# RGCN edge stages: sums carried across tiles, an empty tile between relations, and a scatter-add that waits for the one two ahead

## The chip, the cores and the metric

The kernel runs on one core of a Trainium2 chip. The metric is the device time of one execution in microseconds; lower is better. The engines are TensorE (PE, with its weight loads as PEld), VectorE (DVE), ScalarE (ACT), GpSimd (POOL) and SyncE (SP), which issues the plain DMAs. Indirect DMAs (gathers, scatters, scatter-adds) are issued by GpSimd.

## The reference

There are 10000 nodes with 512 features and 5000 edges. The output is made by four blocks with residual sums: a two-layer relational graph convolution (RGCN), a mixture-of-experts feed-forward block, a four-layer GINE network and a ternary feed-forward block. The change touches the first block alone:

```python
def rgcn_gate_layer(x, row, col, edge_type, basis, att, gate_w, root, bias):
    w = jnp.einsum('rb,bio->rio', att, basis)
    x_j = x[col]
    msgs = []
    for r in range(NUM_RELATIONS):
        gate = jax.nn.sigmoid(x_j @ gate_w[r, :, 0])
        msgs.append(gate[:, None] * x_j @ w[r])
    msg = jnp.where((edge_type == 0)[:, None], msgs[0], msgs[1])
    agg = jax.ops.segment_sum(msg, row, num_segments=x.shape[0])
    return agg + x @ root + bias
...
h = jax.nn.relu(rgcn_gate_layer(x, row, col, edge_type, basis1, att1, gate_w1, root1, bias1))
out = rgcn_gate_layer(h, row, col, edge_type, basis2, att2, gate_w2, root2, bias2)
```

`row` (the input `src`) is the node that an edge adds to, `col` (`dst`) the node whose features it reads; there are two relations and 30 basis matrices of 512x512.

## The kernel before

**Preparation.** `sort_edges` sorts the edges on the chip, once by relation and `src`, the node that an RGCN edge adds to (`by_src`, its table `by_src_d`), and once by `dst`, the node that a GINE edge adds to (`by_dst`). The sorted edges of `by_src` lie in 41 tiles (`RT`) of 128; the second relation starts at a tile's border. Beside the sort the node pass `rgcn_nodes1` normalizes all nodes, multiplies them by the root matrix and writes the result to `r1_d`. `relation_weights` adds the basis matrices up, on DVE (L637).

**Targets.** Within a tile several edges can have the same target. `equal_keys` (L212) compares a tile's 128 keys with each other, and `add_targets` keeps the target's row for the first edge of each key; the others get a spare row of their own behind the nodes (the last 128 rows of `r1_d` and `a2_d`). So a scatter-add never names a node twice. Two neighbouring tiles can name the same node, where a key's edges go over a border.

**The edge stages.** `rgcn_edges` runs twice over the tiles: stage 1 reads the normalized nodes and adds to `r1_d`, stage 2 reads `r1_d` through a ReLU and adds to `a2_d`. For each tile t:
- `fetch`: an indirect gather of 128 node rows into `x` (eight buffers), L614.
- `make_ready`: in stage 2 the ReLU on ACT (L665); two dot products with the gates on DVE (`prod`, L669); a sigmoid on ACT (`g`, L674); the choice by relation on DVE (`dots`, L675); a transpose of the keys on TensorE (`ps_k`, L680); then `same` on DVE (L682), a 128x128 matrix that is the gate where two edges have one key, and zero elsewhere.
- `add_up`: four products of `x` with `same` on TensorE (L689), which add the edges of each key and give the transposed sums; ACT copies them to `aT` (L693). Column j of `aT` is the sum for the key of edge j.
- `put`: the product of `aT` with the relation's weights (L703, eight TensorE instructions in the trace), whose place comes from a register; ACT copies it to `o` (three buffers, L708); GpSimd issues the scatter-add (L619) of `o` to the targets.

The loop runs these staggered, `FETCHED` = 6 and `READY` = 3. In turn i the order is: gather of tile i, `add_up` of tile i-5, `put` of tile i-6, `make_ready` of tile i-3, and then a piece of other work. That other work is the generator `placing` (`place_nodes`): it goes forward by one piece in every second turn of stage 1 and in each turn of stage 2, and ends in stage 2. The orders of PE, GpSimd, ACT and DVE in this loop are those of the code (`manual_schedule`); around it a scheduler decides. Scatter-adds of one stage name the same DRAM tensor, so each waits for the landing of the one before.

When stage 1 has landed, the gathers of stage 2 start; when stage 2 has landed, the first feed-forward block loads `r1_d` and `a2_d`.

`place_nodes` also holds the lines that find, for the sort by `dst`, whether a key goes on into the next tile (`ends`, `carried`); the GINE block carries its sums with them.

Of the kernel before, what the change touches and what calls it, by code (L numbers as in the profile page):

```python
# [8 lines left out]
F32 = mybir.dt.float32  # L9
BF = mybir.dt.bfloat16  # L10
F16 = mybir.dt.float16
I32 = mybir.dt.int32
AF = mybir.ActivationFunctionType
OP = mybir.AluOpType
# [3 lines left out]
P = 128  # L18
N = 10000
D = 512  # L20
KC = D // P
E = 5000
ET = 40
EP = E // ET
SENT = 30000.0
EDGE_SLOTS = ET * P
LO = 256
HI = (N + LO - 1) // LO
RT = ET + 1

PAIRS = [(p * 1024, 512) for p in range(N // 1024)] + [(N // 1024 * 1024, N % 1024 // 2)]
PT = 8
# [13 lines left out]
FETCHED, READY = 6, 3  # L46
# [23 lines left out]
def gnn_ffn_kernel(ctx: ExitStack, tc: tile.TileContext, I, out, dram):  # L70
    nc = tc.nc
# [6 lines left out]


    xn_d = dram("xn_d", [N, D])  # L80
    r1_d = dram("r1_d", [N + P, D])
    a2_d = dram("a2_d", [N + P, D])
    xf_d = dram("xf_d", [N + P, D])
    x2_d = dram("x2_d", [N + P, D])
    xg_d = dram("xg_d", [N, D])
# [41 lines left out]
    nc.vector.memset(eps_t, LN_EPS)  # L127

    def clear_spare(zero, d):
        nc.sync.dma_start(d[N:, :], zero)  # L130


    def rows_to(sb, d, b, store=False):
# [83 lines left out]
    def sort_edges(tag, key_d, partner_d, attr_d, table, wk, ps, keep, by_relation=False):  # L217
# [77 lines left out]
        if by_relation:  # L295

            first_r = wk.tile([P, P], F32, name="first_r")
            nc.vector.tensor_scalar(off[:, 1:2], ip, float(HI), None, op0=OP.is_lt)
            nc.vector.tensor_scalar(first_r, ones, off[:, 1:2], None, op0=OP.mult)
            ps_o = ps.tile([P, LO], F32, name="ps_s")  # L300
            nc.tensor.matmul(ps_o[:hr, :1], lhsT=first_r[:hr, :hr], rhs=total[:hr], start=True, stop=True)
            n_i = wk.tile([P, 3], I32, name="n_i")
            nc.vector.tensor_scalar(n_i[:hr, 0:1], ps_o[:hr, :1], float(P - 1), None, op0=OP.add)
            nc.vector.tensor_scalar(n_i[:hr, 1:2], n_i[:hr, 0:1], 7, None, op0=OP.logical_shift_right)
            nc.vector.tensor_scalar(n_i[:hr, 2:3], n_i[:hr, 1:2], 7, None, op0=OP.logical_shift_left)
            nc.vector.tensor_copy(off[:hr, 1:2], n_i[:hr, 2:3])
            nc.vector.tensor_sub(off[:hr, 1:2], off[:hr, 1:2], ps_o[:hr, :1])
            nc.vector.tensor_scalar(off[:hr, 2:3], ip[:hr], float(HI), None, op0=OP.is_ge)
            nc.vector.tensor_mul(off[:hr, 1:2], off[:hr, 1:2], off[:hr, 2:3])
            nc.vector.tensor_add(off[:hr, 0:1], off[:hr, 0:1], off[:hr, 1:2])  # L310
            nc.vector.tensor_copy(off[:1, 3:4], n_i[:1, 1:2])
            w_at = keep.tile([1, RT], I32, name=f"w_at_{tag}")
            nc.vector.tensor_scalar(
                w_at, irow[:1, :RT], off[:1, 3:4], float(KC * D), op0=OP.is_ge, op1=OP.mult
            )
            meta["w_at"] = w_at

            pad = wk.tile([P, RT + 1, 4], F32, name="pad")
            nc.vector.memset(pad, 0.0)
            nc.vector.memset(pad[:, :, 0], SENT)  # L320
            nc.sync.dma_start(table.rearrange("(p t) c -> p t c", p=P), pad)
# [47 lines left out]
        nc.vector.tensor_copy(gidx, srt[:, :, 1])  # L369
        return dict(meta, key=key, gidx=gidx, attr=srt[:, :, 2])  # L370

    def add_targets(meta, wk, ps, keep):

        key = meta["key"]
        first = wk.tile([P, RT], F32, name="before")
        equal_keys(key, RT, below, first, wk, ps)
        w = wk.tile([P, RT], F32, name="w_se")
        nc.vector.tensor_scalar(first, first, 0.0, None, op0=OP.is_equal)
        nc.vector.tensor_scalar(w, key, float(N), None, op0=OP.is_lt)
        nc.vector.tensor_mul(first, first, w)  # L380
        spare = wk.tile([P, RT], F32, name="spare")
        nc.vector.tensor_scalar(spare, ip.to_broadcast([P, RT]), float(N), None, op0=OP.add)
        nc.vector.tensor_sub(w, key, spare)
        nc.vector.tensor_mul(w, w, first)
        nc.vector.tensor_add(w, w, spare)
        sidx = keep.tile([P, RT], I32, name="sidx")
        nc.vector.tensor_copy(sidx, w)
        return dict(meta, sidx=sidx)

    def place_nodes(meta, wk, ps, keep):  # L390

# [6 lines left out]

        key = meta["key"]
        tno = irow[:, :ET]  # L400

        ends = wk.tile([P, 2, ET], F32, name="ends")
        for i, sel in enumerate((first_sel, last_sel)):
            ps_l = ps.tile([P, LO], F32, name="ps_s")
            nc.tensor.matmul(ps_l[:, :ET], lhsT=sel, rhs=key, start=True, stop=True)
            nc.vector.tensor_copy(ends[:, i], ps_l[:, :ET])
        carried = keep.tile([P, 4, ET], F32, name="carried")
        co, stays, passes, enters = (carried[:, i] for i in range(4))
        nc.vector.memset(carried, 0.0)
        nc.vector.tensor_tensor(co[:, : ET - 1], ends[:, 1, : ET - 1], ends[:, 0, 1:], OP.is_equal)  # L410
        nc.vector.tensor_scalar(stays, co, -1.0, 1.0, op0=OP.mult, op1=OP.add)

        nc.vector.tensor_tensor(passes, ends[:, 0], ends[:, 1], OP.is_equal)
        nc.vector.tensor_mul(passes, passes, co)
        nc.vector.tensor_mul(passes[:, 1:], passes[:, 1:], co[:, : ET - 1])
        nc.vector.tensor_sub(enters[:, 1:], co[:, : ET - 1], passes[:, 1:])
        yield

        ahead = wk.tile([P, ET], F32, name="ahead")
# [198 lines left out]
    def scatter_add(dst, idx, src):  # L618
        return nc.gpsimd.indirect_dma_start(  # L619
            out=dst, out_offset=bass.IndirectOffsetOnAxis(ap=idx, axis=0), in_=src, in_offset=None,  # L620
            compute_op=OP.add,
        )
# [17 lines left out]
    def rgcn_edges(tag, meta, src_d, relu, ws, gate_d, dst_d, beside, take):  # L640

        with ExitStack() as s:
            fix = s.enter_context(tc.tile_pool(name=f"re_fix_{tag}", bufs=1))
            wk = s.enter_context(tc.tile_pool(name=f"re_wk_{tag}", bufs=3))
# [6 lines left out]
            nc.vector.tensor_scalar(of_rel[:, :, 1], meta["attr"], 0.0, None, op0=OP.not_equal)  # L653
            w_all = ws.rearrange("p r w -> p (r w)")

            got, ready, sums = {}, {}, {}

            def fetch(t):
                got[t] = wk.tile([P, D], F32, name="x", bufs=FETCHED + 2)
# [2 lines left out]
            def make_ready(t):  # L662
                x, kt = got[t], meta["key"][:, t : t + 1]
                if relu:
                    nc.scalar.activation(x, x, AF.Relu)  # L665
                dots = wk.tile([P, RELATIONS], F32, name="dots")
                prod = wk.tile([P, D], F32, name="prod", bufs=2)
                for r in range(RELATIONS):
                    nc.vector.scalar_tensor_tensor(  # L669
                        prod, x, 1.0, gate[:, r * D : (r + 1) * D], op0=OP.mult, op1=OP.mult,  # L670
                        accum_out=dots[:, r : r + 1],
                    )
                g = wk.tile([P, RELATIONS + 1], F32, name="g")
                nc.scalar.activation(g[:, :RELATIONS], dots, AF.Sigmoid)  # L674
                nc.vector.scalar_tensor_tensor(  # L675
                    dots, g[:, :RELATIONS], 1.0, of_rel[:, t, :], op0=OP.mult, op1=OP.mult,
                    accum_out=g[:, RELATIONS:],
                )
                ps_k = pk.tile([P, P], F32, name="ps_k")
                nc.tensor.transpose(ps_k, kt.to_broadcast([P, P]), ident)  # L680
                same = wk.tile([P, P], F32, name="same", bufs=4)
                nc.vector.tensor_scalar(same, ps_k, kt, g[:, RELATIONS:], op0=OP.is_equal, op1=OP.mult)  # L682
                ready[t] = same

            def add_up(t):
# [6 lines left out]
                sums[t] = wk.tile([P, KC, P], F32, name="aT")  # L692
                nc.scalar.copy(sums[t], ps_a)  # L693

            def put(t):
                aT = sums.pop(t)
                w0 = nc.values_load(
                    meta["w_at"][:, t : t + 1], engines=(mybir.EngineType.PE,), min_val=0, max_val=KC * D,
                    skip_runtime_bounds_check_because="it is 0 or KC * D by the comparison that makes it",
                )  # L700
                ps_o = po.tile([P, D], F32, name="ps_o")
                for k in range(KC):
                    nc.tensor.matmul(  # L703
                        ps_o, lhsT=aT[:, k, :], rhs=w_all[:, bass.ds(w0 + k * D, D)],
                        start=k == 0, stop=k == KC - 1,
                    )
                o = wk.tile([P, D], F32, name="o")
                nc.scalar.copy(o, ps_o)  # L708
                scatter_add(dst_d, meta["sidx"][:, t : t + 1], o)

            E_ = mybir.EngineType
            with tc.manual_schedule(engines={E_.PE, E_.Pool, E_.Activation, E_.DVE}):
                for i in range(RT + FETCHED):
                    if i < RT:
                        fetch(i)
                    if i >= FETCHED - 1 and i - FETCHED + 1 < RT:
                        add_up(i - FETCHED + 1)
                    if i >= FETCHED:
                        put(i - FETCHED)
                    if READY <= i < RT + READY:  # L720
                        make_ready(i - READY)
                    if take(i):
                        next(beside, None)

# [1149 lines left out]
```

## Time and profile before

| | |
|---|---|
| median of 3 runs | 4619.68 us (4619.44 to 4631.54) |
| the profiled execution | 4620.11 us |
| its span, first to last instruction | 4618.3 us |
| mean granted TensorE clock | 0.937 |
| busy share PE / DVE / ACT / POOL | 87% / 61% / 37% / 34% |
| first gather of stage 1 | 534.3 us |
| first gather of stage 2 | 842.2 us |
| first load of the next block | 1096.2 us |
| scatter-adds | 41 in each stage, 1.58 us (median) each on GpSimd |

The times inside the span are read from the timeline. "Busy" is the time in which an engine ran instructions; a group's row gives the operation, output and inputs, the count, the busy time and the mean, and behind them the idle time before it with what ended it ("<-" names the releaser). A wait's row gives the total wait, the number of waits and the longest. The granted clock is in parts of full speed.

### The profile page before, as it was taken

The numbers are of one execution on the slowest core, as the hardware profiler recorded it, in microseconds if no ns is written. First come the engines' busy times: TensorE is split into PE (matmuls) and PEld (weight loads), VectorE is DVE, ScalarE is ACT, GpSimd is POOL, SyncE is SP. The second block draws the span as 40 slices with busy tenths as digits, with TensorE's granted clock in tenths as the row PEclk, the third lists the DMA queues.
The fourth block names the chain that finished last, engine by engine and source line by source line (L and its number), as shares of the span: only waits on it lengthen the run. The fifth ranks groups of instructions, "written<-read, shape, count | busy, mean of one in ns | idle before, by whom it ended". The sixth has DMA issues, their size and how long they took to land.

```text
span 4618.3 us, 42924 instructions
## 1 busy us (share of the span) xinstructions
PE 4021.0 (87%) x13624; PEld 2037.0 (44%) x13624; DVE 2799.6 (61%) x5886; ACT 1723.0 (37%) x3086; POOL 1548.1 (34%) x1124
## 2 busy tenths in 40 slices
PE   6799568897999953996879999999999999999997
PEld 3443234443444421443444545545455455544443
DVE  7888865553545455655765546654576455755776
ACT  4334112232333311114544523344233532335775
POOL 3434334342000034785563113311142111422443
PEclk9899789898989875998989999999999999999998
DMA  8777755456555422897621123102231012311332
GB/s 281 232 259 248 226 127 89 83 105 169 197 170 182 158 64 59 160 162 208 199 71 51 73 77 116 47 19 80 83 111 38 28 76 107 89 31 48 110 112 97
DMA packets 294560, 558.83 MB, mean 121 GB/s; under 512 B 41376, under 2 KB 72129, under 8 KB 293311
## 3 DMA queue, kind: packets, MB, share of 16 engines
q1 hardware_dynamic: 221072, 367.30, 23.5%
q0 software_dynamic: 73264, 188.79, 17.7%
q8 instruction: 111, 1.82, 0.2%
q14 instruction: 113, 0.93, 0.1%
HBM read 295.03 MB, written 260.95 MB: 120 GB/s over the span
## 4 chain that ended last, share of the span: by engine, by line
PE 37%; DVE 9%; DMA 3%; issue 2%; ACT 2%; POOL 1%; POOLq 0%; DVEq 0%; ACTq 0%; SPq 0%
PE ps_b L1340 15%; PE ps_d L1340 9%; PE ps_o L1646 5%; PE ps_e L1340 4%; PE ps_x L1482 2%; PE ps_x L1268 2%; DVE stats L1455 2%; DMA x<-xg_d,gpos 1%; DVE feat L1272 1%; DMA x_in<-x_d,node_at 1%; PE ps_q L1714 1%; DVE feat L1355 1%; DVE x L1257 1%; DVE t L1386 1%; POOL e L1261 1%
## 5 line engine op out<-in xcount | busy, mean ns | idle before, releaser
L1340 PE MATMUL ps_b<-feat,w 128*128 128x512 f32 (+1 forms) x1120 | 499.1, 588 | 6.9 <-ACT feat L1468 6.9
L1340 PE MATMUL ps_d<-feat,w_s 128*128 128x512 f32 (+1 forms) x1096 | 490.7, 584 | 2.2 <-DVE feat L1387 1.3
L1348 ACT ACTIVATE feat<-ps_b,cols 128x512 f32<-128x512 f32 (+1 forms) x300 | 204.1, 682 | 535.2 <-PE ps_b L1340 522.5
L1394 POOL TENSOR_TENSOR feat<-feat 128x1024 f32<-128x1024 f32 (+1 forms) x70 | 162.7, 2324 | 627.0 <-DVE feat L1393 601.9
L637 DVE SCALAR_TENSOR_TENSOR w<-basis,att,w 128x2048 f32<-128x2048 f32 x116 | 316.3, 2736 | 14.9 <-DMA basis<-in_L_gnn_basis 14.9
L742 PE MATMUL ps_o<-root,xT 128*128 128x512 f32 (+1 forms) x632 | 322.2, 622 | 0.0
L1409 POOL TENSOR_TENSOR feat<-feat,p 128x1024 f32<-128x1024 f32 (+1 forms) x66 | 166.7, 2525 | 449.2 <-ACT feat L1348 449.0
L1340 PEld LDWEIGHTS ps_b<-feat,w 128*128 128x128 f32 x1120 | 209.9, 192 | 240.8 <-issue 209.5
L703 PE MATMUL ps_o<-w,aT 128*128 x656 | 304.1, 608 | 0.0
L1484 DVE TENSOR_TENSOR x_rows<-ps_x,be 128x512 f32<-128x512 f32 (+1 forms) x237 | 157.5, 685 | 232.3 <-PE ps_x L1482 232.0
L918 PE MATMUL ps_n<-root,rT 128*128 128x512 f32 (+1 forms) x632 | 288.9, 613 | 0.0
L1340 PEld LDWEIGHTS ps_d<-feat,w_s 128*128 128x128 f32 x1096 | 198.4, 191 | 194.2 <-issue 173.0
L1340 PE MATMUL ps_b<-t,w_s 128*128 128x512 f32 (+1 forms) x560 | 253.2, 592 | 26.1 <-ACT feat L1348 26.1
L614 POOL DMA_INDIRECT x<-xg_d,gpos x160 | 175.6, 1098 | 260.8 <-PE ps_x L1268 50.8
L1340 PE MATMUL ps_e<-feat,w 128*128 128x512 f32 (+1 forms) x560 | 253.9, 592 | 9.3 <-DVE feat L1303 9.3
L1340 PE MATMUL ps_b<-feat,w_s 128*128 128x512 f32 (+1 forms) x560 | 250.0, 585 | 0.0
L1468 ACT ACTIVATE feat<-feat,bn_sm 128x512 f32<-128x512 f32 (+2 forms) x320 | 238.0, 808 | 3.6 <-DVE bn_sm L1446 3.6
L1455 DVE BATCH_NORM_STATS2 stats<-feat 128x6 f32<-128x512 f32 (+1 forms) x320 | 203.6, 667 | 41.4 <-POOL feat L1409 28.3
L1268 PEld LDWEIGHTS ps_x<-same,x 128*128 128x128 f32 x1280 | 165.5, 197 | 110.7 <-ACT x L1263 48.8
L1268 PE MATMUL ps_x<-same,x 128*128 128x128 f32 x1280 | 172.9, 284 | 46.8 <-ACT x L1263 33.1
L170 DVE BATCH_NORM_STATS2 ln_st<-x_in 128x6 f32<-128x512 f32 (+1 forms) x237 | 159.6, 683 | 63.0 <-DMA x_in<-x_d,node_at 59.0
L1263 ACT ACTIVATE x<-x 128x512 f32<-128x512 f32 x160 | 98.9, 628 | 242.4 <-DVE x L1257 174.2
(492 smaller groups left out, 7649.4 us busy)
## 6 DMA issues: line engine op xcount, KB each, us to landing
basis<-in_L_gnn_basis SPq DMA_DIRECT2D x60, 1024.0 KB
xg_d<-x_rows SPq DMA_DIRECT2D x234, 256.0 KB
xg_d<-x_in SPq DMA_DIRECT2D x39, 512.0 KB
x_in<-in_x SPq DMA_DIRECT2D x19, 1024.0 KB
a_d<-x_in SPq DMA_DIRECT2D x19, 1024.0 KB
xn_d<-xn SPq DMA_DIRECT2D x19, 1024.0 KB
r_d<-o_nodes SPq DMA_DIRECT2D x19, 1024.0 KB
r_in<-r_d SPq DMA_DIRECT2D x19, 1024.0 KB
```

What stands on the lines that cost most here:

```text
L614: return nc.gpsimd.indirect_dma_start(out=dst, out_offset=None, in_=src, in_offset=bass.IndirectOffsetOnAxis(ap=idx, axis=0))
L637: nc.vector.scalar_tensor_tensor(ws[:, r], tf, c, ws[:, r], op0=OP.mult, op1=OP.add)
L703: nc.tensor.matmul(ps_o, lhsT=aT[:, k, :], rhs=w_all[:, bass.ds(w0 + k * D, D)], start=k == 0, stop=k == KC - 1,)
L742: nc.tensor.matmul(ps_o[:n], lhsT=xT[:, k, a * P : a * P + n], rhs=root[:, k, :], start=k == 0, stop=k == KC - 1,)
L918: nc.tensor.matmul(ps_o[:n_], lhsT=rT[:, k, a * P : a * P + n_], rhs=root[:, k, :], start=k == 0, stop=k == KC - 1,)
L1268: nc.tensor.matmul(ps_a[:, k, :], lhsT=x[:, k * P : (k + 1) * P], rhs=same, start=True, stop=True)
L1340: nc.tensor.matmul(ps[fo], lhsT=A[a][:, k, fo * P : (fo + 1) * P], rhs=x[:, k, :], start=first and k == 0, stop=k == 1, skip_group_check=True,
L1348: nc.scalar.activation(dst[:, fo, :], ps[fo], func, bias=b, scale=scale)
L1409: (nc.vector if last else nc.gpsimd).tensor_tensor(b22, b22, p5, OP.add)
L1455: nc.vector.bn_stats(stats[:, k, 2 * p + j, :], big[:, k, s0 + j * w : s0 + (j + 1) * w])
L1468: nc.scalar.activation(hb, hb, AF.Relu, bias=sm[:, fo, 3:4], scale=sm[:, fo, 2:3])
L1646: nc.tensor.matmul(ps_o[:n_], lhsT=big[:, kc, t * P : t * P + n_], rhs=W2[kc], start=kc == 0, stop=kc == KC - 1,)
```

## The change

The scatter-add may now overlap the one before it, and for that two neighbouring tiles must not name the same node. Three things see to it:

- **A carry.** `carries` (moved out of `place_nodes`, with `ends_of`) makes for each tile two factors: `passes` (the key fills the tile and goes on) and `enters` (the first key came from the tile before and ends here). A new step `carry` in the loop takes the last column of `aT`, with what is passed on, as `acc`, and adds what the tile before left over to the first column of `aT`. `add_targets` now gives a key that goes on into the next tile the spare row instead of the node's.
- **An empty tile between the relations**, so that two tiles of one node in different relations don't lie side by side. `RT` becomes 42. Odd and even tiles have their own 128 spare rows, so `r1_d` and `a2_d` have 256, and `clear_spare` clears them in two DMAs.
- **The scatter-add** is declared free of the one before it; it still waits for the one two ahead.

GpSimd is also taken out of the loop's written order, and its instructions are placed by the scheduler.

```diff
-RT = ET + 1
+RT = ET + 2
...
-    r1_d = dram("r1_d", [N + P, D])
-    a2_d = dram("a2_d", [N + P, D])
+    r1_d = dram("r1_d", [N + 2 * P, D])
+    a2_d = dram("a2_d", [N + 2 * P, D])
...
     def clear_spare(zero, d):
-        nc.sync.dma_start(d[N:, :], zero)
+        for r0 in range(N, d.shape[0], P):
+            nc.sync.dma_start(d[r0 : r0 + P, :], zero)
...
-            nc.vector.tensor_scalar(n_i[:hr, 0:1], ps_o[:hr, :1], float(P - 1), None, op0=OP.add)
+            nc.vector.tensor_scalar(n_i[:hr, 0:1], ps_o[:hr, :1], float(2 * P - 1), None, op0=OP.add)
...
+    def ends_of(key, tiles, wk, ps):
+        ends = wk.tile([P, 2, tiles], F32, name="ends")
+        for i, sel in enumerate((first_sel, last_sel)):
+            ps_l = ps.tile([P, LO], F32, name="ps_s")
+            nc.tensor.matmul(ps_l[:, :tiles], lhsT=sel, rhs=key, start=True, stop=True)
+            nc.vector.tensor_copy(ends[:, i], ps_l[:, :tiles])
+        return ends
+
+    def carries(ends, tiles, keep, tag):
+        carried = keep.tile([P, 4, tiles], F32, name=f"carried_{tag}")
+        co, stays, passes, enters = (carried[:, i] for i in range(4))
+        nc.vector.memset(carried, 0.0)
+        nc.vector.tensor_tensor(co[:, : tiles - 1], ends[:, 1, : tiles - 1], ends[:, 0, 1:], OP.is_equal)
+        nc.vector.tensor_scalar(stays, co, -1.0, 1.0, op0=OP.mult, op1=OP.add)
+        nc.vector.tensor_tensor(passes, ends[:, 0], ends[:, 1], OP.is_equal)
+        nc.vector.tensor_mul(passes, passes, co)
+        nc.vector.tensor_mul(passes[:, 1:], passes[:, 1:], co[:, : tiles - 1])
+        nc.vector.tensor_sub(enters[:, 1:], co[:, : tiles - 1], passes[:, 1:])
+        return carried
...
         key = meta["key"]
+        both = wk.tile([P, RT], F32, name="key_rel")
+        nc.vector.tensor_scalar(both, meta["attr"], 0.0, 2.0 * SENT, op0=OP.not_equal, op1=OP.mult)
+        nc.vector.tensor_add(both, both, key)
+        ends = ends_of(both, RT, wk, ps)
+        carried = carries(ends, RT, keep, "s")
         first = wk.tile([P, RT], F32, name="before")
         equal_keys(key, RT, below, first, wk, ps)
         w = wk.tile([P, RT], F32, name="w_se")
+        nc.vector.tensor_tensor(w, both, ends[:, 1], OP.is_equal)
+        nc.vector.tensor_mul(w, w, carried[:, 0])
+        nc.vector.tensor_add(first, first, w)
...
-        nc.vector.tensor_scalar(spare, ip.to_broadcast([P, RT]), float(N), None, op0=OP.add)
+        nc.vector.tensor_scalar(odd, row_i[:, :RT], 1, None, op0=OP.bitwise_and)
+        nc.vector.tensor_copy(spare, odd)
+        nc.vector.tensor_scalar(spare, spare, float(P), ip, op0=OP.mult, op1=OP.add)
+        nc.vector.tensor_scalar(spare, spare, float(N), None, op0=OP.add)
...
+            acc = fix.tile([P, KC], F32, name="acc_0")
+            nc.vector.memset(acc, 0.0)
+            carry_on = {-1: acc}
...
+            def carry(t):
+                aT, last = sums[t], carry_on.pop(t - 1)
+                carry_on[t] = wk.tile([P, KC], F32, name="acc")
+                for dst, src, i in ((carry_on[t], P - 1, 2), (aT[:, :, 0], 0, 3)):
+                    nc.vector.scalar_tensor_tensor(
+                        dst, last, meta["carried"][:, i, t : t + 1], aT[:, :, src], op0=OP.mult, op1=OP.add
+                    )
...
-                scatter_add(dst_d, meta["sidx"][:, t : t + 1], o)
+                st = scatter_add(dst_d, meta["sidx"][:, t : t + 1], o)
+                if stores:
+                    tc.declare_no_dep(st.ins, stores[-1].ins, reason="they have different rows")
+                stores.append(st)
...
-            with tc.manual_schedule(engines={E_.PE, E_.Pool, E_.Activation, E_.DVE}):
+            with tc.manual_schedule(engines={E_.PE, E_.Activation, E_.DVE}):
...
                     if READY <= i < RT + READY:
                         make_ready(i - READY)
+                    if i >= FETCHED - 1 and i - FETCHED + 1 < RT:
+                        carry(i - FETCHED + 1)
                     if take(i):
                         next(beside, None)
```

The work beside comes behind the carry in a turn.

More of the change, by code (lines that the diff above doesn't have):

```diff
@@ L380, in add_targets @@
         nc.vector.tensor_mul(first, first, w)
+        odd = wk.tile([P, RT], I32, name="odd")
         spare = wk.tile([P, RT], F32, name="spare")
-        nc.vector.tensor_scalar(spare, ip.to_broadcast([P, RT]), float(N), None, op0=OP.add)
+        nc.vector.tensor_scalar(odd, row_i[:, :RT], 1, None, op0=OP.bitwise_and)
+        nc.vector.tensor_copy(spare, odd)
+        nc.vector.tensor_scalar(spare, spare, float(P), ip, op0=OP.mult, op1=OP.add)
+        nc.vector.tensor_scalar(spare, spare, float(N), None, op0=OP.add)
         nc.vector.tensor_sub(w, key, spare)
@@ L387, in add_targets @@
         nc.vector.tensor_copy(sidx, w)
-        return dict(meta, sidx=sidx)
+        return dict(meta, sidx=sidx, carried=carried)
     def place_nodes(meta, wk, ps, keep):
@@ L400, in place_nodes @@
         tno = irow[:, :ET]
[L402 to L416, printed above, removed]
+        ends = ends_of(key, ET, wk, ps)
+        carried = carries(ends, ET, keep, "d")
+        co = carried[:, 0]
         yield
@@ L654, in rgcn_edges @@
             w_all = ws.rearrange("p r w -> p (r w)")
-            got, ready, sums = {}, {}, {}
+            got, ready, sums, stores = {}, {}, {}, []
+            acc = fix.tile([P, KC], F32, name="acc_0")
+            nc.vector.memset(acc, 0.0)
+            carry_on = {-1: acc}
             def fetch(t):
```

## The prediction

> **What bounds the kernel now.** I began with the windows view, cut at the borders of the two edge stages. The page's chain of waits says nothing of them: its first piece, listed in order of time, starts at 2081 us. The edge stages run from the first gather (534.3 us) to the last landing of a scatter-add (1096.2 us), 562 us of the 4618.3 us span; before them lie the sort and the node pass, behind them the first feed-forward block.
>
> ```profile
> core 0: us, PE busy (x) PEld busy (x) DVE busy (x) ACT busy (x) POOL busy (x), PEclk, DMA share, GB/s
> ...
> 633.00:842.00 209.00, 173.30 (x653) 93.48 (x651) 99.04 (x377) 44.13 (x103) 89.18 (x66) 0.96 0.49 85
> ...
> 862.00:962.00 100.00, 100.00 (x411) 53.66 (x411) 64.05 (x236) 34.97 (x79) 47.98 (x36) 1.00 0.52 91
> 962.00:1050.00 88.00, 79.06 (x305) 42.06 (x304) 45.18 (x168) 26.89 (x60) 38.69 (x30) 0.96 0.57 110
> 1050.00:1097.00 47.00, 25.42 (x83) 12.60 (x82) 12.12 (x44) 7.62 (x16) 13.71 (x9) 0.78 0.42 63
> ```
>
> Each row is a stretch: its length, then each engine's busy time, the granted clock, DMA. TensorE is full for the first 100 us of stage 2, then less and less. Stage 2's waits tell why:
>
> ```profile
> DVE prod L669 <- ACT x L665: 54.7, 30, 4.3
> ACT o L708 <- DMA a_d<-o,sidx: 50.4, 20, 5.7
> ```
>
> The product of tile t+1 starts 5.12 us after that of tile t; a scatter-add starts only every 5.65 us, since each waits for the landing of the one before. The lag grows until the three buffers `o` are full (about 965 us); from there the scatter-adds set the pace. Here is one tile of stage 2 in the timeline while TensorE still sets it:
>
> ```profile
> 908.59 3.60 PE L703 MATMUL ps_o<-w,aT 128*128 x8
> ...
> 912.27 0.59 ACT L708 COPY o<-ps_o 128x512 f32<-128x512 f32 x1 [1.77 <-issue]
> ...
> 912.75 0.63 ACT L665 ACTIVATE x<-x 128x512 f32<-128x512 f32 x1
> ...
> 913.41 0.69 DVE L669 SCALAR_TENSOR_TENSOR prod<-x,gate 128x512 f32<-128x512 f32 x1 [1.35 <-ACT x L665]
> 913.60 0.30 PEld L703 LDWEIGHTS ps_o<-w,aT 128*128 128x128 f32 x2
> 913.71 3.60 PE L703 MATMUL ps_o<-w,aT 128*128 x8
> ...
> 914.15 0.69 DVE L669 SCALAR_TENSOR_TENSOR prod<-x,gate 128x512 f32<-128x512 f32 x1
> ...
> 914.94 0.20 ACT L674 ACTIVATE g<-dots 128x2 f32<-128x2 f32 x1 [1.56 <-DVE prod L669]
> ...
> 915.17 0.20 DVE L675 SCALAR_TENSOR_TENSOR dots<-g,of_rel 128x2 f32<-128x2 f32 x1 [0.33 <-ACT g L674]
> ...
> 915.49 0.41 DVE L682 TENSOR_SCALAR same<-ps_k,key_s,g 128x128 f32<-128x128 f32 x1
> ```
>
> Read it as a chain that starts at a product and ends at `same`: product, copy `o`, ReLU, two dot products, sigmoid, `dots`, `same`. ACT and DVE take their work in the written order, so `same` of tile i-3 comes 7 us behind the start of the product of tile i-6. This costs nothing today: `same` is read two turns later, and the next product (913.71) does not wait for it.
>
> **The change, part by part.**
>
> *The carry* is the part that decides. It adds two small DVE instructions to each tile, written behind `same` in the same turn, and they write the first column of `aT`, which the next turn's product reads. In the built order the product has a new wait on DVE, behind a register load; queued behind it on TensorE are the key transpose, the beside work and the next sums, and for these DVE waits in turn. So the slack of two turns is gone and the chain closes to a loop: product, `o`, (ReLU), dots, sigmoid, `same`, carry, next product.
> Stage 2, from the rows above: product to `o` 3.68, to ReLU 0.48, to the first `prod` 0.66, to the second 0.74, to sigmoid 0.79, to `dots` 0.23, to `same` 0.32, to the next DVE instruction 0.33 (at 905.21 `same` is followed at 905.54). The carry has no row; the nearest is `dots`, the same kind of instruction on 128x2, at 0.16 each, and small DVE work starts 0.1 apart, so 0.27 for both (bounds 0.2 and 0.5). From DVE's end to the weight load and the product 0.16 (DVE end 1054.76, weight load 1054.81, 0.11 more to the matmul). Sum 7.66; with the semaphore and register load now exposed I take 7.7 (7.5 to 8.0).
> Stage 1 has no ReLU and its dots run beside the product: 3.68 + 0.49 + 0.23 + 0.28 + 0.33 + 0.27 + 0.16 = 5.44, taken as 5.5. There the product now starts after 4.44 at best, 6.95 in turns where four tiles of `equal_keys` lie beside.
>
> *The scatter-add waits for the one two ahead.* This ends the 5.65 us pace: two in flight allow one per 2.8 us, and GpSimd needs 1.58 + 0.30 + 1.0 + 0.30 = 3.2 us per tile. But at 7.7 us per turn nobody waits for it; only the lag at the ends is won. Before, TensorE's last product of stage 2 ends at 1074.25 and the next block's first load starts at 1096.18; after, 0.08 + 0.59 + 0.28 + 5.5 = 6.45 us lie between. The weight preparation in that gap takes 10.8 us from 1074.3, and the next block's TensorE starts 7.3 us behind its first load (1103.49), so it stays covered. Were that cover gone, 4 us.
>
> *GpSimd's order is no longer written by hand.* Ten gathers now come before the first scatter-add and three more stay ahead throughout. A gather needs its buffer back from the sums of eight tiles ago, which TensorE does just before the product whose scatter-add stands behind that gather, so it holds nothing: 0.
>
> *One tile more* per stage (42), the empty one: one turn each.
>
> *Preparation* (0 to 534 us): 19 more DVE instructions, three TensorE ones; such rows take 0.17 to 0.19, so at most 3.6 us on a DVE that is 81% busy there. Two more clears on SP's queue (0.33 us each to issue, 0.25 MB each, 1 us at that stage's 250 GB/s) and three small column loads moved back. The order is otherwise nearly the old one. I take +3 (-3 to +6).
>
> *TensorE's clock.* The loop leaves a gap of about 2.5 us in each stage-2 turn (7.7 less the 5.12 of work). What a gap does, the timeline shows at 765 us:
>
> ```profile
> 762.77 0.27 PE L680 MATMUL ps_k<-ident,key_s 128*128 128x128 f32 x1
> 765.33 0.62 PE L488 MATMUL ps_s<-incl_p,less_next 40*41 40x256 f32 x2 [2.29 <-DVE less_next L486]
> ...
> 765.93 1.88 PE L689 MATMUL ps_a<-same,x 128*128 128x128 f32 x8
> 767.60 4.58 PE L703 MATMUL ps_o<-w,aT 128*128 x8
> ```
>
> After 2.29 us without work the product took 4.58 us, not 3.60, and the sums 1.88, not 1.06. The Trainium skill ("TensorE: Matmul & The Clock Gate", "HAM oscillation — how this bites in real kernels") gives the rule of no TensorE gaps above about 3.4 us; by it these gaps would cost nothing, and the sum below would be 15 smaller. By the row each can cost 1.0 (1.7 after the 3.97 us gap at 741, where the product took 5.29). Over the whole timeline 18 gaps of 2.0 to 2.5 us begin at full clock and 7 are followed by half clock (the clock's record moved 10.7 us earlier, where it fits the slow products). So 39 x 7/18 x 1.0 = +15; ends 0 and 39 x 1.7 = 66.
>
> **Sum for stage 1** (534 to 842.2). First six products, while DVE still builds weights: DVE is full in both, +5 (0 to 12). Then 16 short turns of 4.44 become 5.5: +17. Eighteen long ones get the carry's 0.25: +4.5. Turns with heavy DVE work beside (`passed` 3.5 and its reduction 3.4, the scans) used the lost slack: +8 (2 to 12). One turn more: +5.5. Lag at the end: 826.45 to 842.2 is 15.8, becomes 6.45: -9.3. Together +31.
>
> **Sum for stage 2** (842.2 to 1096.2, 254.0 us). After: 14.2 + 0.6 to the first product, 39 turns x 7.7 = 300.3, two last turns without dots 8.9, the last product 3.6, 6.45 to the landing: 334. So +80.
>
> All: 3 + 31 + 80 + 15 = +129. The profiled execution took 4620.1 us (span 4618.3 and 1.8 around it), the median of the runs is 4619.7. 4619.7 + 129 = 4749.
>
> **The rivals.**
> *The pace was the scatter-add's, and the carry hides* (not slower). If the product did not meet the carry, stage 2 would run at TensorE's own pace: 14.2 + 29 x 5.12 + 10 x 4.44 + 8.9 + 3.6 + 6.45 = 226, -28; stage 1 -9.3 + 4.4 = -5; preparation +3: 4590 us. For it speaks the 50.4 us that ACT waits for the scatter's landing. It decides where `o` to carry takes at most 5.12 - 3.68 = 1.4 us; the rows give 4.0, and the carry is written behind `same`. Chance 0.04.
> *Every gap cools TensorE.* +66 instead of +15 gives 4800; 2.5 us is above the 2.29 that cooled it, but 11 of 18 such gaps didn't. Chance 0.13.
> *The change doesn't do what it says*, the scatter-add still waits for its neighbour. In the built order it waits for the second one back. Were it otherwise, 5.65 fits in 7.7, and the time would hardly differ.
>
> **How the numbers follow.** Forecast 0.82, cooling 0.13, not slower 0.04; 0.01 for a result near zero. The low end takes preparation 0, stage 1 +10, stage 2 +72 (7.5 a turn), clock 0: +80, so 4700. The high end takes +6, +42, +88 and +50: 4806. A measurement of this kernel tells 0.3% (14 us) from no change, and the forecast's whole range lies above that: slower 0.95, same 0.01, faster 0.04.
>
> **What would show it.** In the profile after: products of stage 2 start 7.7 us apart, TensorE is two thirds busy there, its wait before the product (or before the weights) ends on the carry's DVE row, `o` waits no more for the scatter-add's landing, and the last landing follows the last product by 6 to 7 us. Stage 1's short turns are near 5.5. I am wrong if products of stage 2 stay below 6 us apart, or if the preparation ends more than 10 us away from 534.

## The result and the profile after

The changed kernel takes **4794.34 us** (median of 4 runs, 4790.19 to 4809.47). The kernel before took 4625.61 us beside it (4 runs, 4619.44 to 4632.85). The ratio is **1.037, with a 95% interval of 1.034 to 1.040**: slower by about 169 us. The profiled execution took 4795.35 us, its span is 4793.5, and the mean granted clock of TensorE is 0.930 (0.937 before).

Cut at the same borders as before (first gather of stage 1, first gather of stage 2, first load of the next block), the loss lies in the two edge stages. Each figure is a difference of two such times in one profiled execution:

| us | before | after | difference |
|---|---|---|---|
| preparation | 534.3 | 542.8 | +8.5 |
| stage 1 | 307.9 | 352.4 | +44.5 |
| stage 2 | 254.0 | 375.0 | +121.0 |
| everything behind | 3522.1 | 3523.3 | +1.2 |

The windows view of the changed kernel, cut at the long middle part of stage 1 and at the turns of stage 2 (columns as before):

```profile
core 0: us, PE busy (x) PEld busy (x) DVE busy (x) ACT busy (x) POOL busy (x), PEclk, DMA share, GB/s
...
652.00:889.00 237.00, 188.08 (x650) 102.21 (x650) 106.11 (x439) 44.11 (x104) 85.93 (x64) 0.94 0.42 72
...
910.00:1255.00 345.00, 244.44 (x789) 122.09 (x790) 129.25 (x516) 70.46 (x157) 94.24 (x72) 0.89 0.33 60
```

In stage 2 TensorE was fully busy at first; now it is busy for 244 of 345 us, at a granted clock of 0.89, and no other engine is near full. A stage in which everybody has time is one in which the engines wait for each other in turn. The waits from 910 to 1250 us (total, times, longest):

```profile
POOL a_d L643 <- ACT o L745: 234.9, 39, 7.9
DVE prod L698 <- ACT x L694: 191.6, 39, 6.7
ACT o L745 <- issue: 188.9, 35, 6.2
PEld ps_o L740 <- ACT aT L722: 100.5, 37, 3.3
PE ps_o L740 <- DVE aT L728: 94.6, 38, 3.1
```

The product (L740) waits for the carry (L728), once per turn. The wait of `o` for the scatter-add's landing, 50.4 us before, has no row any more, and GpSimd waits longer for `o` (234.9 us; 78.8 before). One turn of stage 2 in the timeline shows the loop, from one product to the next but one:

```profile
973.15 3.67 PE L740 MATMUL ps_o<-w,aT 128*128 x8 [2.41 <-DVE aT L728]
...
976.90 0.59 ACT L745 COPY o<-ps_o 128x512 f32<-128x512 f32 x1 [4.41 <-issue]
...
977.38 0.64 ACT L694 ACTIVATE x<-x 128x512 f32<-128x512 f32 x1
...
978.05 0.69 DVE L698 SCALAR_TENSOR_TENSOR prod<-x,gate 128x512 f32<-128x512 f32 x1 [3.73 <-ACT x L694]
...
978.78 0.69 DVE L698 SCALAR_TENSOR_TENSOR prod<-x,gate 128x512 f32<-128x512 f32 x1
...
979.58 0.20 ACT L703 ACTIVATE g<-dots 128x2 f32<-128x2 f32 x1 [1.56 <-DVE prod L698]
...
979.81 0.16 DVE L704 SCALAR_TENSOR_TENSOR dots<-g,of_rel 128x2 f32<-128x2 f32 x1 [0.33 <-ACT g L703]
...
980.09 0.41 DVE L711 TENSOR_SCALAR same<-ps_k,key_s,g 128x128 f32<-128x128 f32 x1
980.42 0.21 DVE L728 SCALAR_TENSOR_TENSOR acc<-acc,carried_s,aT 128x4 f32<-128x4 f32 x1
980.55 0.22 DVE L728 SCALAR_TENSOR_TENSOR aT<-acc,carried_s,aT 128x4 f32<-128x4 f32 x1
...
980.91 5.37 PE L740 MATMUL ps_o<-w,aT 128*128 x8 [2.41 <-DVE aT L728]
...
990.38 3.67 PE L740 MATMUL ps_o<-w,aT 128*128 x8 [2.41 <-DVE aT L728]
```

Two things are to be seen. The chain is the one that the prediction listed, `same` at its end and the carry behind it, and the next product starts 7.76 us after the first. But the product at 980.91 takes 5.37 us instead of 3.67, so its turn takes 9.47; the granted clock over this turn is 0.82, and 1.00 over a short one (929.00 to 936.72 us). Of the 39 turns of stage 2, from 910.14 to 1251.02 us, 22 take 9.4 us or more and the other 17 stay between 7.7 and 8.1.

### The profile page after: what moved, and what is told of

Read it like the earlier page. It is cut to its first block, busy times and chain, and to the rows that moved or that the text cites. A ratio compares the mean times of both kernels' runs of the same rounds, so it can differ in the third digit from the quotient of the medians.

```text
span 4793.5 us, 43321 instructions
## 1 busy us (share of the span) xinstructions
PE 4101.3 (86%) x13663; PEld 2070.9 (43%) x13663; DVE 2824.5 (59%) x6089; ACT 1725.8 (36%) x3093; POOL 1553.7 (32%) x1128
## 3 DMA queue, kind: packets, MB, share of 16 engines
q1 hardware_dynamic: 221360, 367.82, 22.7%
## 4 chain that ended last, share of the span: by engine, by line
PE 37%; DVE 8%; DMA 3%; ACT 2%; issue 2%; POOL 1%; POOLq 0%; DVEq 0%; ACTq 0%
PE ps_b L1382 14%; PE ps_d L1382 8%; PE ps_o L1688 4%; PE ps_e L1382 4%; PE ps_x L1524 2%; PE ps_x L1310 2%; DMA x<-xg_d,gpos 1%; DVE stats L1497 1%; DMA x_in<-x_d,node_at 1%; PE ps_q L1756 1%; DVE feat L1314 1%; ACT feat L1510 1%; DVE feat L1397 0%; DVE x L1299 0%; POOL e L1303 0%
## 5 line engine op out<-in xcount | busy, mean ns | idle before, releaser
L740 PE MATMUL ps_o<-w,aT 128*128 x672 | 364.4, 693 | 151.1 <-DVE aT L728 147.1
L661 DVE SCALAR_TENSOR_TENSOR w<-basis,att,w 128x2048 f32<-128x2048 f32 x116 | 329.6, 2853 | 14.7 <-DMA basis<-in_L_gnn_basis 14.7
L740 PEld LDWEIGHTS ps_o<-w,aT 128*128 128x128 f32 x672 | 142.2, 222 | 318.6 <-issue 191.0
L698 DVE SCALAR_TENSOR_TENSOR prod<-x,gate 128x512 f32<-128x512 f32 x168 | 115.8, 689 | 206.1 <-ACT x L694 197.2
```

The lines of the kernel that those rows point to most:

```text
L661: nc.vector.scalar_tensor_tensor(ws[:, r], tf, c, ws[:, r], op0=OP.mult, op1=OP.add)
L740: nc.tensor.matmul(ps_o, lhsT=aT[:, k, :], rhs=w_all[:, bass.ds(w0 + k * D, D)], start=k == 0, stop=k == KC - 1,)
```

## The experiments

The experiments ran in three batches, each on a chip of its own. The kernel before took 4600.65 us (23 runs) in the first (carry first, neighbour wait, gap filled, tiles only), 4622.29 us (23 runs) in the second (carry first with neighbour wait, copy last, after once more), and 4620.93 us (one run) in the third (before once more, gap half filled). So kernels are compared by their ratios and by the lengths of the stages.

The times in the expectations go by a kernel before of about 4620 us. On the first batch's chip it is 20 us faster, so hold that batch against its expectations as ratio times 4620: 4609 us (carry first), 4800 (neighbour wait), 4761 (gap filled), 4645 (tiles only). All four lie in the ranges that the theory gave.

These are the lengths, in us, in the profiled execution of each kernel, and the ratio to the kernel before with its interval:

| | preparation | stage 1 | stage 2 | ratio |
|---|---|---|---|---|
| before (first profile) | 534.3 | 307.9 | 254.0 | 1 |
| before, once more | 532.7 | 309.2 | 254.4 | |
| after (first profile) | 542.8 | 352.4 | 375.0 | 1.037 [1.034, 1.040] |
| after, once more | 540.0 | 350.7 | 374.9 | 1.0381 [1.0363, 1.0398] |
| carry first | 538.0 | 307.6 | 227.7 | 0.9977 [0.9969, 0.9985] |
| neighbour wait | 540.8 | 353.8 | 377.9 | 1.0389 [1.0369, 1.0410] |
| gap filled | 549.2 | 350.6 | 342.1 | 1.0306 [1.0284, 1.0329] |
| gap half filled | 547.4 | 349.4 | 347.9 | |
| tiles only | 549.2 | 318.3 | 262.3 | 1.0055 [1.0035, 1.0075] |
| carry first, neighbour wait | 542.0 | 318.3 | 260.3 | 1.0062 [1.0044, 1.0079] |
| copy last | 546.9 | 306.0 | 229.1 | 0.9984 [0.9975, 0.9994] |

**The carry ahead of the preparation.** Only the place of the call in the turn changes.

```diff
                     if i >= FETCHED:
                         put(i - FETCHED)
+                    if i >= FETCHED - 1 and i - FETCHED + 1 < RT:
+                        carry(i - FETCHED + 1)
                     if READY <= i < RT + READY:
                         make_ready(i - READY)
-                    if i >= FETCHED - 1 and i - FETCHED + 1 < RT:
-                        carry(i - FETCHED + 1)
```

> The carry of a tile is written ahead of the dot products of the same turn instead of behind them; nothing else differs from the changed kernel. Theory A (the loss is the loop product - o - ReLU - dots - sigmoid - same - carry - next product, closed by the carry's place in DVE's order): the loop opens, products of stage 2 start 5.12 us apart while other work lies beside and 4.44 after that, the cold products vanish, stage 2 takes about 228 us instead of 375 and the kernel 4600 us (4585 to 4620). Theory B (the carry's own cost, two scatter-adds in flight, or GpSimd's new order makes the turn long): it stays above 4750 us.

Measured: 4591.86 us (20 runs, 4579.41 to 4598.62), a ratio of 0.9977. Stage 2 fell from 375.0 to 227.7 us and stage 1 from 352.4 to 307.6. Its timeline, two products of stage 2 with what lies between on DVE's side:

```profile
974.12 3.60 PE L740 MATMUL ps_o<-w,aT 128*128 x8
...
975.87 0.41 DVE L711 TENSOR_SCALAR same<-ps_k,key_s,g 128x128 f32<-128x128 f32 x1
976.19 0.47 DVE L591 TENSOR_SCALAR_CACHE_REDUCE waste_p<-ps_r,wanted 128x256 bf16<-128x256 f32 x1
...
977.52 0.21 DVE L728 SCALAR_TENSOR_TENSOR acc<-acc,carried_s,aT 128x4 f32<-128x4 f32 x1
...
977.65 0.21 DVE L728 SCALAR_TENSOR_TENSOR aT<-acc,carried_s,aT 128x4 f32<-128x4 f32 x1
...
979.24 3.60 PE L740 MATMUL ps_o<-w,aT 128*128 x8
```

The carry now starts 1.72 us before the product that needs it, behind the other work of the turn before, and the product no longer waits. Turns are 5.12 us while other work lies beside, and TensorE is busy for 193.6 of 194 us (866 to 1060); every product behind the first takes 3.60 or 3.67. The same instructions with the same data dependences cost nothing that shows in this place: the place in DVE's order, not the carry's work, made the loss. This version is a little faster than the kernel before too: 0.2%, with an interval of 0.9969 to 0.9985.

**The loop cut on ScalarE.** The carry stays last; the copy of `o` and the scatter-add move behind `make_ready`.

```diff
                     if READY <= i < RT + READY:
                         make_ready(i - READY)
+                    if i >= FETCHED:
+                        put_out(i - FETCHED)
                     if i >= FETCHED - 1 and i - FETCHED + 1 < RT:
                         carry(i - FETCHED + 1)
```

Here `put` ends with the product, and `put_out` holds the copy of `ps_o` to `o` and the scatter-add.

> The carry stays where the change put it, last in the turn, behind the selection matrix; instead ScalarE copies the product out of PSUM (and the scatter is issued) after the preparation of tile t+3, not before it. The theory (a loop: product, copy of o, ReLU, dots, sigmoid, selection matrix, carry, next product): cutting it on ScalarE works as well as on DVE, for the ReLU no longer waits for the product of its own turn; turns of 5.1 us with products of 3.6, stage 2 about 228 to 235 us, the ratio 0.997 to 1.003. The rival: the carry's place on DVE alone costs the time, for the product needs a carry that waits for dots and sigmoid whatever ScalarE's order is: turns stay at 7.76 and 9.46 us, stage 2 near 375, ratio near 1.037.

Measured: 4614.59 us (20 runs), a ratio of 0.9984, stage 2 at 229.1 us. The theory's figures are met, the rival's are not. The timeline of this kernel:

```profile
981.54 3.60 PE L740 MATMUL ps_o<-w,aT 128*128 x8
...
982.28 0.63 ACT L694 ACTIVATE x<-x 128x512 f32<-128x512 f32 x1
...
985.22 0.59 ACT L749 COPY o<-ps_o 128x512 f32<-128x512 f32 x1 [0.55 <-PE ps_o L740]
...
985.75 0.22 DVE L728 SCALAR_TENSOR_TENSOR aT<-acc,carried_s,aT 128x4 f32<-128x4 f32 x1
...
986.66 3.60 PE L740 MATMUL ps_o<-w,aT 128*128 x8
```

The ReLU starts 0.74 us behind the start of the product, not after its end, and so everything down to the carry fits beside the product. The carry is still the last step behind `same`, and the turn is 5.12. So it is a loop, and cutting either of two links opens it: ScalarE's written order (copy of `o` ahead of the ReLU) was as much a link as DVE's.

**The scatter-add waits for its neighbour again**, all else as in the changed kernel.

```diff
                 st = scatter_add(dst_d, meta["sidx"][:, t : t + 1], o)
-                if stores:
-                    tc.declare_no_dep(st.ins, stores[-1].ins, reason="they have different rows")
```

> The changed kernel, but each scatter-add waits for the one just before it again. Theory A: a turn of 7.76 us or more covers the 5.65 us of a scatter-add, so only the last two or three tiles of each stage feel it: 4798 us (4790 to 4808). Theory B (two scatter-adds in flight get in each other's way): faster than the changed kernel by more than 10 us, under 4784.

Measured: 4780.68 us, a ratio of 1.0389 [1.0369, 1.0410], where the changed kernel has 1.0381 [1.0363, 1.0398] in the second batch. The intervals overlap, so by the time the new freedom of the scatter-add makes no difference that can be told in the closed loop. By the stages it is 3 us in each, and in stage 2 they lie at the end: from the last product's end to the next block's first load it is 9.4 us instead of 6.1.

**Carry first and the neighbour's wait together**, to see what that freedom is worth in the open loop. It is the first experiment with the three lines of the one above taken out.

> The carry ahead of the preparation as in e1_carry_first, and every scatter waits again for the one before it. The theory: in the changed kernel this wait had no effect only because a closed loop of 7.76 us and more per turn covered it; with the loop open the scatters, 5.65 us apart in the kernel before, set the turn again. Stage 2 then takes about 262 us and stage 1 about 318, as in e4_tiles_only (no carry, neighbour wait), instead of 228 and 308: a ratio to before near 1.006, some 40 us above e1_carry_first. The rival: that gain of e1 over e4 came from GpSimd's issue order being free, or from the missing carry's place, and the wait is worth nothing anywhere: stage 2 stays near 228 us and the ratio near 0.998.

Measured: 4650.58 us, a ratio of 1.0062 against 0.9977 without the wait. Of the 43 us by which the two stages are longer (318.3 against 307.6, and 260.3 against 227.7), stage 2 has 32.6. Among its waits in stage 2:

```profile
ACT o L745 <- DMA a_d<-o,sidx: 51.7, 19, 6.3
```

The row of before (50.4 us, 20 times, longest 5.7) is back. So the freed scatter-add does what it says and is worth about 40 us, once nothing slower stands over it.

**The tile and the preparation alone**: no carry in the loop, each scatter-add waits for the one before, GpSimd's order written by hand again. The kernel leaves the carry out, so sums that go over a border are not completed.

```diff
-                if stores:
-                    tc.declare_no_dep(st.ins, stores[-1].ins, reason="they have different rows")
...
-            with tc.manual_schedule(engines={E_.PE, E_.Activation, E_.DVE}):
+            with tc.manual_schedule(engines={E_.PE, E_.Pool, E_.Activation, E_.DVE}):
...
-                    if i >= FETCHED - 1 and i - FETCHED + 1 < RT:
-                        carry(i - FETCHED + 1)
```

> All of the change's preparation and its 42 tiles, but no carry step in the loop (sums that go over a tile's border are left out), scatter-adds wait for their neighbour, and GpSimd's order is written by hand as before. Theory: one turn more in each stage (5.6 us each) and a preparation that ends 8.5 us later, 4640 us (4632 to 4648). If the later end of the preparation was chance in one execution: 4631 us. Theory B (tiles or preparation cost more than the loop): above 4680.

Measured: 4629.11 us, a ratio of 1.0055. Stage 1 is 10.4 us longer than before, stage 2 8.3. That is some 25 us of the loss by the ratio, and the rest needs the carry in its place. It also tells why the carry first gains so little on the kernel before: the tile and the preparation take back most of the scatter-add's 40 us. Beside it stands the kernel with the carry first and the neighbour's wait: it has the carry and GpSimd's free order in addition, and its stages are as long (318.3 and 260.3). So neither the carry's work nor GpSimd's free order costs anything that shows.

**The gap ahead of the product filled**, in stage 2 only: two products of weights by weights, whose result the real product overwrites.

```diff
                 ps_o = po.tile([P, D], F32, name="ps_o")
+                if relu:
+                    for _ in range(2):
+                        nc.tensor.matmul(ps_o, lhsT=w_all[:, :P], rhs=w_all[:, :D], start=True, stop=True)
```

> The changed kernel, with two products of the weights with themselves ahead of each product of stage 2, into the same PSUM tile, which the product then overwrites: 1.7 us of work without a wait in the 2.4 us gap. Clock theory (every second product is slow because TensorE's clock fell in the gap): all products of stage 2 take 3.67 us, turns are 7.76 us, and the kernel is 37 us faster, 4757 us (4748 to 4768). If the slow products have another cause, or the gap is needed whole: 4794 us or more.

Measured: 4745.74 us, a ratio of 1.0306; stage 2 took 342.1 us, 32.9 less than in the changed kernel. TensorE in the timeline:

```profile
969.46 1.88 PE L741 MATMUL ps_o<-w 128*128 128x512 f32 x4
972.04 3.67 PE L743 MATMUL ps_o<-w,aT 128*128 x8 [0.69 <-DVE aT L728]
...
977.23 1.88 PE L741 MATMUL ps_o<-w 128*128 128x512 f32 x4
979.80 3.67 PE L743 MATMUL ps_o<-w,aT 128*128 x8 [0.69 <-DVE aT L728]
```

Work added to the kernel made it faster. Products still start 7.76 us apart, since the loop is untouched, but each takes 3.67, at a granted clock of 1.00 from 925 to 1220 us (0.89 there in the changed kernel): the slow products came from the gap.

**Half the filling**: one such product (`range(1)`), meant to leave 1.55 us. One execution, for its profile.

> The changed kernel with one product of weights by weights in the gap ahead of each product of stage 2, where e3_fill_gap had two: the gap that remains is about 1.6 us instead of 0.7 (2.41 without any). If the clock falls after a gap of some 2.4 us only, every product takes 3.67 us and stage 2 takes 342 us, as with two. If the share of idle time in the turn decides, some of the products still take 5.4 us: stage 2 lies between 342 and 375 us.

Measured: stage 2 took 347.9 us (the kernel 4780.17 us in this one execution, the kernel before 4620.93). Its timeline:

```profile
1014.54 3.67 PE L743 MATMUL ps_o<-w,aT 128*128 x8 [1.55 <-DVE aT L728]
...
1022.71 5.37 PE L743 MATMUL ps_o<-w,aT 128*128 x8 [1.96 <-DVE aT L728]
...
1032.18 3.67 PE L743 MATMUL ps_o<-w,aT 128*128 x8 [1.56 <-DVE aT L728]
...
1179.85 5.37 PE L743 MATMUL ps_o<-w,aT 128*128 x8 [2.24 <-DVE aT L728]
...
1189.31 5.37 PE L743 MATMUL ps_o<-w,aT 128*128 x8 [2.24 <-DVE aT L728]
...
1198.78 3.67 PE L743 MATMUL ps_o<-w,aT 128*128 x8 [2.23 <-DVE aT L728]
```

Four of its 39 turns took 9.47 us, against 22 without filling and none with two products of filling; a fifth slow product ends the row. The gap was not 1.55 us throughout. Thirty products had gaps of 1.50 to 1.90 us ahead of them, and none was slow; the one at 1022.71 had 1.96, and the last eight, beside which the other work has ended, had 2.23 or 2.24. Of these nine, five were slow. So a gap somewhat shorter than 2.4 us can be followed by a slow product, which the first branch of the expectation left out. That the idle share of the turn decides is not shown by it: the turns are all about 7.77 us long, so a longer gap is a larger share as well.

**Both kernels once more**, for the preparation.

> The changed kernel once more, on the chip of the experiments: a ratio of 1.037 as before, stage 2 near 375 us and stage 1 near 352. The time to the first gather of stage 1 (542.8 us in its first profile, 538 to 549 in the experiments, 534.3 before) shows whether the 8 us of the preparation belong to the change or differ from one execution to the next.

> The kernel before once more, for its own sections beside those of the experiments: about 308 us from the first gather of stage 1 to that of stage 2, 254 us from there to the next block's first load. Its first gather stood at 534.3 us in its one profile, and at 538 to 549 us in the seven profiles of kernels with the changed preparation. If those milliseconds belong to the change, it stands near 534 again; if the end of the preparation differs from one execution to the next, it can stand anywhere up to 549.

("Milliseconds" in the second is a slip for microseconds.) Measured: the changed kernel has the ratio 1.0381 and the same stages within 2 us. The first gather came at 532.7 us in the second profile of before (534.3 in the first), and at 538.0 to 549.2 us in the nine profiles of kernels with the changed preparation, 544.0 in the mean. So the preparation's loss belongs to the change, some 10 us with a spread as large as itself.

## Why the prediction was right or wrong

The forecast was 4749 us in a range of 4700 to 4806; it came to 4794. The side and the mechanism were right, and the miss of 45 us is in the sizes of three terms, above all the clock's. (By the medians side by side the change is 169 us, where 129 was forecast. The low end of the range is out by 2 us in itself: its parts add up to +82, not +80.)

- **The carry closes a loop: right.** Predicted 7.7 us per warm turn, measured 7.76. The parts fit too: product to `o` 3.75 (3.68 predicted), both carries 0.26 from start to start (0.27), DVE's next start to the product 0.23 (0.16). The two experiments that cut the loop show that it is one.
- **Stage 2 without the clock: right.** 14.9 us to the first product (14.8), 39 turns, 6.1 us from the last product's end to the next block's first load (6.45). Of the 121.0 us, 22 slow products at 1.7 are 37.4; the other 83.6 stand against the predicted 80.
- **TensorE's clock: the term that was mis-sized.** Predicted 39 x 7/18 x 1.0 = 15 us; the run has 22 x 1.7 = 37, and filling the gap gave back 33. Both factors were too small: 22 of 39 instead of 7 of 18, and 1.7 instead of 1.0. The 7 in 18 were counted over the whole timeline of before; here a gap comes in every turn. Whether that is why more of them are followed by slow products was not tested. The skill's rule of 3.4 us would have made it nothing; the trace had already spoken against it, and the runs do so more strongly: no gap of these 39 is longer than 3.1 us. The rival "every gap cools" came near the total with 4800, but by the wrong division: it wanted 39 slow turns, 22 came, and the rest of the miss lies elsewhere.
- **Stage 1: +44.5 instead of +31.** Short turns 5.50 (5.5 predicted) and the end (6.4 instead of 15.8 us, so -9.4; predicted -9.3) are right. Two terms were too small. From the first gather to the seventh product it is +10.5 instead of +5: the carry now stands in the DVE queue where that queue is full of weight sums, and the first product starts 34.2 us behind the first gather instead of 22.7 (22.5 with the carry first). From there to the last product it is +43.4 (189.5 to 232.9) instead of 17 + 4.5 + 8 + 5.5 = 35. Of these 8 us some 6 can be products at a low clock (over this stretch the excess above the usual 3.6 or 3.67 sums to 3 us before and 8.5 after, if each delays the loop in full): the prediction's clock term looked at stage 2 only. Long turns went from 6.95 to 7.28, 0.33 instead of 0.25. The rest I can't divide.
- **The scatter-add two ahead wins only the ends: right in this kernel.** Its worth of about 40 us in the open loop is beyond what the prediction asked; but the prediction's rival "the carry hides" put stage 2 at 226 us, and the version with the carry first has 227.7.
- **GpSimd's order: 0, and nothing shows.** For one tile more the prediction took one turn in each stage, 5.5 and 7.7 us. Tiles alone made the stages 10.4 and 8.3 us longer; what of this is the tile was not divided.
- **Preparation: +3 predicted (-3 to +6), +8.5 in the profile.** What the trace shows is the end of the node pass: its last two stores stand on SP's queue behind loads of `basis`, which wait for DVE's weight sums. They were issued at 523.59 us before and at 533.30 after, and the first gather starts 10.7 and 9.5 us behind that (before, its wait ends on the landing of `r_d<-o_nodes`):

```profile
527.59 0.46 SPq L140 DMA_DIRECT2D r_d<-o_nodes  x1
532.88 0.37 SPq L654 DMA_DIRECT2D basis<-in_L_gnn_basis  x1
533.30 1.12 SPq L140 DMA_DIRECT2D r_d<-o_nodes  x2
```

The prediction counted 19 instructions at their own length, and looked at DVE's work alone, not at when the node pass ends. The queue is not the whole of it: GpSimd's last addition of the node pass, which the last store writes, also ends later, at 528.2 us instead of 514.0. What shifts the node pass was not tried by itself and stays open.

## What to carry to other kernels

Before a step is written into an in-order turn, follow the chain from the consumer back to itself through every engine's written order: here a 0.2 us instruction that was one place too late turned two turns of slack into a loop of 7.76 us, and one moved call took the whole change from 3.7% slower to 0.2% faster than the kernel before. A relaxed wait has its worth only while nothing slower stands over it, so try it in the open loop before it is called useless. A loop that leaves TensorE idle in each turn can pay twice, once for the gap and once for slow products after it; an added dummy product shows the second part by itself.

## What the hardware showed that was not expected

About every second product behind a gap of 2.36 to 3.1 us was slow, 5.37 us instead of 3.67: 22 of 39 in both profiles of the changed kernel, for long stretches in strict alternation. With half the filling none of 30 was slow behind 1.50 to 1.90 us, and 5 of 9 behind 1.96 to 2.24; with the whole filling, which leaves 0.65 to 1.38 us, none of 39. From about 2 us on a longer gap was no worse: 16 of 28 were slow behind 2.36 to 2.6 us, 4 of 8 behind 2.9 to 3.1. The Trainium skill ("TensorE: Matmul & The Clock Gate", "Part 1: The HAM clock gate (the "warmup" mystery)") says that the clock follows how busy TensorE has been over a free-running window. That would let the same gap be followed by a slow product at one time and not at another, as seen here; but no run shows the window itself, and none tells the length of the gap from its share of the turn. Why the slow products alternate was not tested.
